# A sign convolution on four 64x64 array tiles, half-image layout and folded norms in a convolution-attention kernel

## The chip, the core and the metric

The kernel runs on one core of one Trainium2 chip. The metric is the time of one execution on the device in microseconds (us), median of several. The engines are TensorE (PE; its weight loads are listed as PEld), VectorE (DVE), ScalarE (ACT), GpSimd (POOL) and SyncE (SP), which issues the DMAs. Each executes its own queue in order and waits for the others by semaphores.

## The reference

Sixteen images of 256 channels and 56x56 positions pass through two layers. `_gn` normalises groups of 8 channels over all positions.

```python
# layer 0: x = x + conv_block(_gn(x))
xq = sign(xn + bias)
out = 0
for i, d in enumerate((1, 3, 5)):                # three dilations
    wq = scale * sign(w[i] - mean(w[i]))         # one scale and mean per output channel
    y = conv3x3(xq, wq, dilation=d, groups=4)    # 64 channels in, 64 out, per group
    y = y + cb[i] - move1[i]
    out += where(y >= 0, y, alpha[i] * y) + move2[i]
out = (out - mean_c(out)) * rsqrt(var_c(out) + 1e-5) * gamma + beta   # over channels
# layer 1: x = x + attention(_gn(x))
q, k, v = 1x1 convolutions of xn, 64 channels each (8 heads of 8)
k, v = unfold3x3(k) + depthwise3x3(k) + biases, same for v            # 9 neighbours
att = softmax over the 9 neighbours of sum_c(q * k)
out = proj(sum over neighbours of att * v), 64 -> 256 channels
```

## The kernel before

An image lies in SBUF as two chunks of 128 channels (`KC`), 3136 positions each, in f32. `front` (L228) takes the group statistics of an image, writes (x - mean) * r on DVE (L238) and its sign on ACT (L246) into two zero-bordered bf16 images `sgn`. `layer0` goes through 7 tiles of 8 rows (448 positions). `conv_tile` (L249) makes, for each chunk and dilation, 9 matmuls (one a tap, L263) of a 128x128 block-diagonal weight matrix (two of the four groups) into one PSUM bank; ACT evacuates it twice with Relu (`up` L272, `dn` L276), DVE combines these into the PReLU (L279), and POOL adds the three dilations (L283, L284). `post` works one tile behind: `centre` (L286) makes the channel mean with a 1/256 matrix (`lmp` L291), subtracts it (L295), squares on ACT (L299) and sums the squares into one row of a PSUM bank for up to four tiles (`lvp` L300). After the fourth and the seventh tile `residual` (L308) takes the root of a 4x448 tile (L199 to L205), spreads each row over 128 partitions by a matmul (`lrp` L315), multiplies (L317), applies gamma and beta on ACT (L318), adds to the image on POOL (L326) and takes the statistics for layer 1 (L328).

`qkv_tile` (L360) normalises the image again on DVE (L365) and makes q, k and v (`qps` L378) with the top half of the image on partitions 0 to 63 and the bottom half on 64 to 127; ACT evacuates (L387, L392). `layer1` has 7 tiles of 4 rows in each half. `attn_weights` multiplies q with 9 shifted k (L412, two on DVE and one on POOL), makes the scores (`lg` L427) and the softmax; `attn_out` transposes (`tp` L454), copies (`at` L460), makes the weights of the shifted v (`ap` L467), multiplies with v (L477), adds on POOL (L491 to L493), projects (`op` L498) and adds to the image (L507).

All PSUM tiles come from one pool of 8 banks (`bank`). Tile pools set how many buffers of a kind there are: 3 images, 6 `ct`, 10 `y` (448 columns, used by nine kinds of tile), 6 `p`. The instructions are put into each engine's queue by a planner, which follows the order of the program by priority and puts an instruction earlier where it expects an engine to wait. An f32 matmul appears in the trace as two passes, each with its weight load.

The images are one layer apart. In step b the program has, in order: load of image b+2, `layer0` of image b+1 (with the q/k/v of image b put in ahead of the last tile's norm), `front` of image b+2, and `layer1` of image b with its store.

Of the kernel before, what the change touches and what calls it, by code (L numbers as in the profile page):

```python
# [7 lines left out]
F32 = mybir.dt.float32  # L8
# [5 lines left out]
P = 128  # L14
C, H, W = 256, 56, 56
HW = H * W
KC = C // P                 # channel chunks of 128
DIL = (1, 3, 5)
PADC = 5                    # zero border of the sign image: the largest dilation
HP = H + 2 * PADC  # L20
TR = 8                      # image rows of a convolution tile
TN = TR * W                 # 448 positions
NT = H // TR                # 7 tiles
LNB = 4                     # tiles whose channel-norm variances are worked on together
NH, CH = 8, 8               # attention heads, channels of a head
D = NH * CH                 # 64
HH = H // 2                 # rows of a half image: partitions 0-63 hold the top half, 64-127 the bottom
AR = 4                      # rows of an attention tile, in each half
AN = AR * W                 # 224 positions
NAT = HH // AR              # 7 tiles  # L30
BN = 2 * W                  # 112 positions: one stationary block of the scores' product
HJ = NH * 9                 # 72 scores of one position
# [4 lines left out]
# columns of the packed per-channel parameters  # L37
# [4 lines left out]
def _view(ap, dims, offset=0):  # L42
    """The partitions of `ap` with other free dimensions (step, count), from its start on."""
    return bass.AP(ap.tensor, ap.offset + offset, [ap.ap[0], *dims])
# [3 lines left out]
def preact_conv_attention(  # L48
# [4 lines left out]
    par: bass.AP,  # L53
    wqkv: bass.AP,
# [8 lines left out]
    bsel: bass.AP,  # L63
# [11 lines left out]
    xpool = ctx.enter_context(tc.tile_pool(name="x", bufs=3))  # L75

    def load(b):
        xt = xpool.tile([P, KC, HW], F32, tag="x", name="xt")
        for k in range(KC):
            nc.sync.dma_start(  # L80
                out=xt[:, k, :], in_=x[b, k * P : (k + 1) * P].rearrange("p h w -> p (h w)")
            )
        return xt

    # ------------------------------------------------------------------ constants and weights
    cst = const.tile([P, 3 * P + LNB * LNB], F32, name="cst")
    nc.sync.dma_start(out=cst, in_=consts)
    ident = cst[:, 0:P]
    gmat = cst[:, P : 2 * P]            # 1/8 within a group of 8 channels
    cmean = cst[:, 2 * P : 3 * P]       # 1/256 everywhere  # L90
    vsel = [cst[:, 3 * P + LNB * t : 3 * P + LNB * (t + 1)] for t in range(LNB)]
    bsl = const.tile([LNB, LNB, P], F32, name="bsl")
    nc.sync.dma_start(out=bsl, in_=bsel)
    pr = const.tile([P, KC, NPAR], F32, name="pr")
    nc.sync.dma_start(out=pr, in_=par)

    images = {0: load(0)}

    wq = const.tile([P, KC, 3, D], F32, name="wq")
# [7 lines left out]
    wp = const.tile([P, C], F32, name="wp")  # L107
    nc.sync.dma_start(out=wp, in_=wproj)

    wconv = const.tile([P, KC, 3, 9, P], BF16, name="wconv")  # L110
    csc = const.tile([P, KC, 3], F32, name="csc")       # weight scale, and its negative
    ncsc = const.tile([P, KC, 3], F32, name="ncsc")
    cbi = const.tile([P, KC, 3], F32, name="cbi")       # cb - move1, and its negative
    ncbi = const.tile([P, KC, 3], F32, name="ncbi")
    nalpha = const.tile([P, KC, 3], F32, name="nalpha")
    mv2 = const.tile([P, KC], F32, name="mv2")          # sum of move2, less its channel mean
    qbs = const.tile([P, 1], F32, name="qbs")
    wmean = const.tile([P, KC, 3], F32, name="wmean")

    nc.vector.tensor_scalar(qbs, qb[:, 0:1], SCALE, None, ALU.mult)  # L120
# [7 lines left out]
    for k in range(KC):  # L128
        nc.tensor.matmul(
            out=m2p[:, 0:1], lhsT=cmean, rhs=mv2[:, k : k + 1], start=k == 0, stop=k == KC - 1  # L130
        )
    nc.vector.tensor_tensor(mv2, mv2, m2p[:, 0:1].broadcast_to([P, KC]), ALU.subtract)

    with tc.tile_pool(name="prep", bufs=2) as prep:
        # taps + identity (unfold and depthwise convolution are one 9x9 map per channel), biases
# [10 lines left out]
        # binary weights: signs (exact in bf16) as block-diagonal [in, out] matrices, and scales  # L146
        for k in range(KC):
            for d in range(3):
                wt = prep.tile([P, D, 9], F32, name="wt")
                nc.sync.dma_start(  # L150
                    out=wt, in_=w[d, k * P : (k + 1) * P].rearrange("o i a b -> o i (a b)")
                )
                wm = wmean[:, k, d : d + 1]
                nc.vector.tensor_reduce(wm, wt, AX.XY, ALU.add, negate=True)
                nc.vector.tensor_scalar(wm, wm, 1.0 / (D * 9), None, ALU.mult)
                ws = csc[:, k, d : d + 1]
                nc.vector.tensor_reduce(ws, wt, AX.XY, ALU.add, apply_absolute_value=True)
                nc.vector.tensor_scalar(ws, ws, 1.0 / (D * 9), None, ALU.mult)
                wz = prep.tile([P, 9, P], F32, name="wz")
                nc.gpsimd.memset(wz, 0.0)  # L160
                for g in range(2):
                    r = slice(g * D, (g + 1) * D)
                    nc.scalar.activation(
                        wz[r, :, r],
                        wt[r].rearrange("o i t -> o t i"),
                        AF.Sign,
                        bias=wmean[r, k, d : d + 1],
                    )
                for t in range(9):
                    tp = bank("wtp")  # L170
                    nc.tensor.transpose(tp[:, 0:P], wz[:, t, :], ident)
                    nc.vector.tensor_copy(wconv[:, k, d, t, :], tp[:, 0:P])
        nc.vector.tensor_scalar(ncsc, csc, -1.0, None, ALU.mult)

    # ------------------------------------------------------------------ working memory
# [10 lines left out]
    cpool = ctx.enter_context(tc.tile_pool(name="c", bufs=6))  # L186
    ypool = ctx.enter_context(tc.tile_pool(name="y", bufs=10))
    ppool = ctx.enter_context(tc.tile_pool(name="p", bufs=6))
    apool = ctx.enter_context(tc.tile_pool(name="a", bufs=2))
    small = ctx.enter_context(tc.tile_pool(name="small", bufs=3))  # L190
    rowp = ctx.enter_context(tc.tile_pool(name="row", bufs=1))

    def ytile(name):
        return ypool.tile([P, TN], F32, tag="y", name=name)

    def rsqrt(pool, v, shape, name):
        """v ** -0.5 for v > 0: square root and reciprocal, then a Newton step to fp32's precision."""
        s = pool.tile(shape, F32, name=f"{name}_s")
        nc.scalar.activation(s, v, AF.Sqrt)  # L199
# [8 lines left out]
    def group_stats(st):  # L208
        """Mean and 1/sqrt(var + eps) of each channel's group, from the channels' bn_stats."""
        mv = small.tile([P, KC, 2], F32, name="mv")  # L210
        for k in range(KC):
            nc.vector.bn_aggr(mv[:, k, :], st[:, k].rearrange("p t s -> p (t s)"))
# [444 lines left out]
```

## Time and profile before

| what | before |
|---|---|
| median of 3 runs | 4715.27 us (4707.69 to 4717.31) |
| span of the profiled execution | 4708.0 us |
| its time outside the span, against the median | about 7 us |
| PE busy | 3666.5 us (78%), 20346 matmul passes |
| DVE / ACT / POOL busy | 2431.7 / 1661.7 / 1552.5 us |
| mean granted TensorE clock | 0.823 |
| convolution matmuls, L263 | 6048, busy 1282.2 us |
| evacuations L272 and L276 | 672 each, busy 485.8 and 480.9 us |
| DMA | 110.36 MB, mean 23 GB/s |

"Busy" is the time in which an engine executes at least one instruction; a wait inside its queue is not busy. A page has six parts: busy shares, the span in 40 slices (digits are tenths), DMA queues, the chain that ended last (followed back from the last instruction), the costliest groups of instructions by line, and DMA issues. The granted clock is the share of full speed that TensorE had; in the trace it is either 1.0 or 0.5 at any time.

### The profile page before, as it was taken

To read this page: it belongs to the slowest core of one execution; us is meant where nothing else is said; L and a number is where in the kernel's file an instruction comes from. 1 tells how busy PE (TensorE), PEld (TensorE's weight loads), DVE (VectorE), ACT (ScalarE), POOL (GpSimd) and SP (SyncE) were. 2 spreads that over 40 slices of the span, in tenths; PEclk is the share of its full clock that TensorE was granted. 3 is DMA by queue.
4 is the path that set the end of the run, shared out by engine and by line. 5 is a ranking of instruction groups with operands and counts; after the bars stand their busy time and mean duration, and the time that the engine had idled before them with its cause. 6 is when DMAs were issued, how large, how long until landed. Compare 5 with 4: busy or idle time off the path is not lost.

```text
span 4708.0 us, 52461 instructions
## 1 busy us (share of the span) xinstructions
PE 3666.5 (78%) x20346; PEld 2262.1 (48%) x20346; DVE 2431.7 (52%) x4472; ACT 1661.7 (35%) x2747; POOL 1552.5 (33%) x1358
## 2 busy tenths in 40 slices
PE   5786877878787787877878778787787877868786
PEld 3345445453553635535354453544545445454565
DVE  6555464554645455464554645546455464553543
ACT  5551441514325153241523505234152441514310
POOL 2333333233333333323333233333333333332333
PEclk8897887978888787887978879788797877978887
DMA  3000101001010010100101001010000101000000
GB/s 118 1 1 1 55 1 55 1 1 55 1 55 1 1 55 1 55 1 1 55 1 55 1 13 43 1 55 1 34 22 1 55 1 55 1 1 28 1 28 28
DMA packets 11657, 110.36 MB, mean 23 GB/s; under 512 B 1532, under 2 KB 2044, under 8 KB 3216
## 3 DMA queue, kind: packets, MB, share of 16 engines
q1 hardware_dynamic: 11408, 107.01, 5.7%
q8 instruction: 160, 2.62, 0.2%
q14 instruction: 89, 0.73, 0.0%
HBM read 55.63 MB, written 51.38 MB: 23 GB/s over the span
## 4 chain that ended last, share of the span: by engine, by line
PE 64%; DVE 16%; POOL 11%; ACT 5%; issue 2%; DMA 0%; POOLq 0%; ACTq 0%; DVEq 0%; SPq 0%
PE cps L263 23%; PE lg L427 14%; PE ap L467 7%; POOL m L491 6%; PE qps L378 5%; PE op L498 4%; PE lvp L300 4%; PE lrp L315 3%; DVE up L279 3%; DVE l_r L201 2%; POOL xt L326 2%; POOL m L492 2%; POOL m L493 2%; DVE m L477 2%; DVE p L412 1%
## 5 line engine op out<-in xcount | busy, mean ns | idle before, releaser
L263 PE MATMUL cps<-sgn,wconv 128*128 128x448 bf16 x6048 | 1282.2, 372 | 8.4 <-ACT sgn L246 8.4
L263 PEld LDWEIGHTS <-wconv 128*128 128x128 bf16 x6048 | 594.1, 100 | 745.1 <-issue 209.0
L279 DVE SCALAR_TENSOR_TENSOR up<-dn,nalpha,up 128x448 f32<-128x448 f32 x672 | 510.7, 766 | 748.2 <-ACT dn L276 745.1
L272 ACT ACTIVATE up<-cps,cbi,csc 128x448 f32<-128x448 f32 x672 | 485.8, 723 | 654.0 <-PE cps L263 653.5
L427 PE MATMUL lg<-wk,p 128*112 128x144 f32 x4032 | 676.3, 334 | 0.9 <-DVE p L412 0.9
L427 PEld LDWEIGHTS lg<-wk,p 128*112 128x112 f32 x4032 | 640.8, 216 | 44.9 <-issue 43.6
L467 PE MATMUL ap<-at,wv 72*64 72x224 f32 x4480 | 558.9, 415 | 73.9 <-ACT at L460 73.9
L460 ACT COPY at<-tp 72x448 f32<-72x448 f32 x112 | 59.1, 527 | 1503.8 <-PE tp L454 1503.8
L283 POOL TENSOR_TENSOR up<-up 128x448 f32<-128x448 f32 x224 | 264.6, 1181 | 902.6 <-DVE up L279 897.6
L498 PE MATMUL op<-m,wp 64*128 64x224 f32 x896 | 209.0, 615 | 372.2 <-POOL m L493 372.2
L276 ACT ACTIVATE dn<-cps,ncbi,ncsc 128x448 f32<-128x448 f32 x672 | 480.9, 716 | 0.0
L467 PEld LDWEIGHTS ap<-at,wv 72*64 72x64 f32 x4480 | 364.2, 160 | 243.0 <-ACT at L460 103.0
L491 POOL TENSOR_TENSOR m<-m 128x448 f32<-128x448 f32 x336 | 379.5, 1129 | 213.3 <-DVE m L477 200.4
L326 POOL TENSOR_TENSOR xt<-xt,ct 128x896 f32<-128x896 f32 x112 | 231.2, 2083 | 650.2 <-ACT ct L318 650.2
L477 DVE TENSOR_TENSOR m<-ap,vt 128x448 f32<-128x448 f32 (+1 forms) x560 | 319.9, 571 | 208.5 <-PE ap L467 171.1
L507 DVE SCALAR_TENSOR_TENSOR xt<-op,pr,xt 128x224 f32<-128x224 f32 x448 | 170.9, 445 | 485.5 <-PE op L498 485.5
L412 POOL TENSOR_TENSOR p<-qt,kt 128x672 f32<-128x672 f32 x112 | 178.8, 1596 | 702.0 <-PE lg L427 643.6
L315 PE MATMUL lrp<-l_r,bsl 4*128 4x448 f32 x224 | 178.4, 970 | 214.0 <-DVE l_r L205 214.0
L498 PEld LDWEIGHTS op<-m,wp 64*128 64x128 f32 x896 | 134.2, 319 | 433.1 <-POOL m L493 427.0
L412 DVE TENSOR_TENSOR p<-qt,kt 128x672 f32<-128x672 f32 x224 | 194.7, 908 | 278.8 <-PE lg L427 159.3
L284 POOL TENSOR_TENSOR ct<-up 128x448 f32<-128x448 f32 x224 | 261.4, 1167 | 141.7 <-DVE up L279 138.6
L378 PE MATMUL qps<-n,wq 128*64 128x224 f32 x2688 | 273.8, 355 | 17.1 <-DVE n L365 17.1
(89 smaller groups left out, 3410.1 us busy)
## 6 DMA issues: line engine op xcount, KB each, us to landing
xt<-in_x SPq DMA_DIRECT2D x32, 1568.0 KB, 9.9
out<-xt SPq DMA_DIRECT2D x32, 1568.0 KB, 5.2
wt<-in_w SPq DMA_DIRECT2D x6, 288.0 KB, 3.3
wk<-in_wk_a SPq DMA_DIRECT2D x1, 720.0 KB, 11.2
kb<-in_wk_b SPq DMA_DIRECT2D x1, 720.0 KB, 12.6
cst<-in_consts SPq DMA_DIRECT2D x1, 200.0 KB
wq<-in_wqkv SPq DMA_DIRECT2D x1, 192.0 KB, 10.1
wv<-in_wv_a SPq DMA_DIRECT2D x1, 180.0 KB
```

Of the source, the lines that this page charges most:

```text
L263: nc.tensor.matmul(out=ps[:, 0:TN], lhsT=wconv[:, k, d, tap, :], rhs=sgn[k][:, r0 : r0 + TR, c0 : c0 + W], start=tap == 0, stop=tap == 8,)
L272: nc.scalar.activation(up, ps[:, 0:TN], AF.Relu, bias=cbi[:, k, d : d + 1], scale=csc[:, k, d : d + 1])
L276: nc.scalar.activation(dn, ps[:, 0:TN], AF.Relu, bias=ncbi[:, k, d : d + 1], scale=ncsc[:, k, d : d + 1])
L279: nc.vector.scalar_tensor_tensor(up, dn, nalpha[:, k, d : d + 1], up, ALU.mult, ALU.add)
L326: nc.gpsimd.tensor_tensor(xv, xv, ct, ALU.add)
L378: nc.tensor.matmul(out=ps[s * D : (s + 1) * D, 0:AN], lhsT=wq[:, k, j, :], rhs=xn[k][:, s * AN : (s + 1) * AN], start=k == 0, stop=k == KC ...
L412: eng.tensor_tensor(p3.rearrange("p d (h w) -> p d h w", w=W), q3.rearrange("p d (h w) -> p d h w", w=W), k3, ALU.mult,)
L427: nc.tensor.matmul(out=lg[0:BN, b * 2 * HJ : (b + 1) * 2 * HJ], lhsT=lhs, rhs=wk[:, j, :], start=j == 0, stop=j == 9,)
L467: nc.tensor.matmul(out=ap[s * D : (s + 1) * D, i * AN : (i + 1) * AN], lhsT=wv[:, j + i, :], rhs=at[:, s * AN : (s + 1) * AN], start=True, ...
L477: nc.vector.tensor_tensor(m[:, 0 : n * AN].rearrange("p (i h w) -> p i h w", h=AR, w=W), ap[:, 0 : n * AN].rearrange("p (i h w) -> p i h w ...
L491: nc.gpsimd.tensor_tensor(ms[0], ms[0], m, ALU.add)
L498: nc.tensor.matmul(out=op[:, k * AN : (k + 1) * AN], lhsT=wp[s * D : (s + 1) * D, k * P : (k + 1) * P], rhs=ms[0][s * D : (s + 1) * D, 0:A ...
```

## The change

*Convolution.* The image is now worked on in strips of 7 rows in both halves (2 x 392 positions), four strips an image. Per chunk, dilation and tap there are four matmuls of 64x64 weights: two groups (rows 0 to 63 or 64 to 127 of the array) times two image halves (columns, so partitions 0 to 63 or 64 to 127 of the output). The result has a group on 128 partitions = 2 halves x 64 channels, so `ct` and the image for the residual are `[128, 4 groups, 1568]`.

*Two copies of the image.* `load_chunks` brings the image by channel chunk for `front`; `load_halves` brings it by half for the residual, after the store of the image whose buffer it takes.

*Norms.* `front` takes the sign of x plus a per-channel shift directly. `layer0` scales the q/k/v weights by the group norm's r and makes a bias from the mean, so `qkv_tile` reads the image itself.

*Channel norm.* Each strip has its own: variances come with positions on the partitions (98 x 8), the root is a power on POOL with a Newton step on DVE, and it is spread by a matmul with the identity.

*Projection.* One 128x128 block-diagonal matmul per group of 64 output channels replaces two 64x128 ones per half.

```diff
-    xpool = ctx.enter_context(tc.tile_pool(name="x", bufs=3))
+    npool = ctx.enter_context(tc.tile_pool(name="xn", bufs=2))
+    xpool = ctx.enter_context(tc.tile_pool(name="x", bufs=2))
...
-    cpool = ctx.enter_context(tc.tile_pool(name="c", bufs=6))
-    ypool = ctx.enter_context(tc.tile_pool(name="y", bufs=10))
-    ppool = ctx.enter_context(tc.tile_pool(name="p", bufs=6))
+    cpool = ctx.enter_context(tc.tile_pool(name="c", bufs=2))
+    upool = ctx.enter_context(tc.tile_pool(name="u", bufs=4))
+    dpool = ctx.enter_context(tc.tile_pool(name="d", bufs=3))
+    qpool = ctx.enter_context(tc.tile_pool(name="q", bufs=1))
+    mpool = ctx.enter_context(tc.tile_pool(name="m", bufs=5))
+    ppool = ctx.enter_context(tc.tile_pool(name="p", bufs=4))
...
     def rsqrt(v, shape, name):
-        s = pool.tile(shape, F32, name=f"{name}_s")
-        nc.scalar.activation(s, v, AF.Sqrt)
-        nc.vector.reciprocal(r, s)
+        nc.gpsimd.tensor_tensor(r, v, h, ALU.pow)        # h: -0.5, broadcast
         nc.vector.tensor_tensor(s, r, r, ALU.mult)
         nc.vector.tensor_tensor(s, s, v, ALU.mult)
         nc.vector.tensor_scalar(s, s, -0.5, 1.5, ALU.mult, ALU.add)
         nc.vector.tensor_tensor(r, r, s, ALU.mult)
...
     def front(xs):
+        # sh = var * r * bias - mean
         for k in range(KC):
-            for t in range(NT):
-                nc.vector.tensor_scalar(n, xt[...], mean, r, ALU.subtract, ALU.mult)
-                nc.scalar.activation(sgn[k][...], n, AF.Sign, bias=pr[:, k, P_BIAS : P_BIAS + 1])
+            for s in range(2):
+                nc.scalar.activation(
+                    sgn[k][:, PADC + s * HH : PADC + (s + 1) * HH, PADC : PADC + W],
+                    xs[k][:, s * HN : (s + 1) * HN].rearrange("p (h w) -> p h w", w=W),
+                    AF.Sign, bias=sh[:, k : k + 1])
...
+    def conv_strip(t):
         for k in range(KC):
             for d, dil in enumerate(DIL):
-                ps = bank("cps")
+                ps = [bank("cps") for _ in range(2)]
                 for tap in range(9):
+                    for j, s in ((0, 0), (1, 1), (0, 1), (1, 0)):
+                        r0 = PADC + s * HH + t * SR + (tap // 3 - 1) * dil
+                        nc.tensor.matmul(
+                            out=ps[j][s * GC : (s + 1) * GC, 0:SN],
+                            lhsT=wconv[j * GC : (j + 1) * GC, k, d, tap, :],
+                            rhs=sgn[k][j * GC : (j + 1) * GC, r0 : r0 + SR, c0 : c0 + W],
+                            start=tap == 0, stop=tap == 8)
+                for j in range(2):
+                    # Relu up, Relu dn on ACT and the PReLU on DVE, per bank of 128x392
             nc.gpsimd.tensor_tensor(es[0], es[0], es[1], ALU.add)               # 128x784
+            nc.gpsimd.tensor_tensor(ct[:, 2 * k : 2 * k + 2, :], es[0], es[2], ALU.add)
...
+    def channel_norm(ct, t, xt, st):
+        # mean: 4 matmuls with 1/256 within a half; 4 subtractions on DVE
+        nc.scalar.activation(sq, ct, AF.Square)                                 # 128x1568
+        for i in range(NVB):                                                    # 4 blocks of 98
+            for g in range(NG):
+                nc.tensor.matmul(out=vp[0:VB, 2 * i : 2 * i + 2],
+                    lhsT=sq[:, g, i * VB : (i + 1) * VB], rhs=hsel, ...)
+        nc.vector.tensor_scalar(v, vp[0:VB, 0 : 2 * NVB], EPS_LN, None, ALU.add)
+        r = rsqrt(v, [VB, 2 * NVB], "l")
+        nc.vector.tensor_copy(rr, r broadcast to [VB, 2 * NVB, GC])
+        for i in range(NVB):
+            nc.tensor.matmul(out=rp[:, i * VB : (i + 1) * VB],
+                lhsT=rr[:, i], rhs=ident[0:VB, 0:VB], start=True, stop=True)
+        nc.vector.tensor_tensor(ct, ct, rp broadcast over 4 groups, ALU.mult)
+        # gamma and beta: 4 on ACT; add to the image on POOL, 128x1568; 4 bn_stats
...
     def layer0(xt, before_tail=None):
+        for t in range(NS):
+            ct = conv_strip(t)
+            if t == NS - 1 and before_tail:
+                before_tail()
+            if last is not None:
+                channel_norm(last, t - 1, xt, st)
+            last = ct
+        channel_norm(last, NS - 1, xt, st)
+        mean, _, r = group_stats(st, NG, gmat1)
+        for g in range(NG):
+            nc.gpsimd.tensor_scalar(wf[:, g], wq[:, g], r[:, g : g + 1], 0.0, ALU.mult, ALU.add)
+        # bp: 24 matmuls of wf (64 columns) with half the mean; bf = qb - bp
...
+    def qkv_tile(xt, wf, bf, t):
+        for g in range(NG):
+            for s, j in ((0, 0), (1, 0), (0, 1), (1, 1)):        # q and k: four 64x64 tiles
+                nc.tensor.matmul(out=pq[s][c * D : (c + 1) * D, 0:AN],
+                    lhsT=wf[s * GC : (s + 1) * GC, g, j, :], rhs=xt[s * GC : (s + 1) * GC, g, pos], ...)
+        for g in range(NG):
+            for s in range(2):                                   # v: two 64x64 tiles
+                nc.tensor.matmul(out=pv[s][s * D : (s + 1) * D, 0:AN], ...)
+        # six evacuations of 64x224 on ACT
...
-        for s in range(2):
+        for g0 in range(0, NG, 2):
             op = bank("op")
-            for k in range(KC):
+            for i in range(2):
                 nc.tensor.matmul(
-                    lhsT=wp[s * D : (s + 1) * D, k * P : (k + 1) * P],
-                    rhs=ms[0][s * D : (s + 1) * D, 0:AN],
+                    lhsT=wp[:, g0 + i, :],
+                    rhs=ms[0][:, 0:AN],
...
         layer1(b, xt)
+        if b + 2 < NB:
+            images[b + 2] = load_halves(b + 2)
```

The preparation also transposes the sign weights four to a bank, copies only their 64x64 blocks, and brings the weight scales into the half layout by eight small DMAs.

## The prediction

> **What bounds the kernel now.** I read the page first: which engine is full, and whether one is full all the time.
>
> ```profile
> PE 3666.5 (78%) x20346; PEld 2262.1 (48%) x20346; DVE 2431.7 (52%) x4472; ACT 1661.7 (35%) x2747; POOL 1552.5 (33%) x1358
> PEclk8897887978888787887978879788797877978887
> PE 64%; DVE 16%; POOL 11%; ACT 5%; issue 2%; DMA 0%; POOLq 0%; ACTq 0%; DVEq 0%; SPq 0%
> PE cps L263 23%; PE lg L427 14%; PE ap L467 7%; POOL m L491 6%; PE qps L378 5%; PE op L498 4%; PE lvp L300 4%; PE lrp L315 3%; DVE up L279 3%; DVE l_r L201 2%; POOL xt L326 2%; POOL m L492 2%; POOL m L493 2%; DVE m L477 2%; DVE p L412 1%
> ```
>
> TensorE carries the chain, but convolution matmuls are only 23% of it, so halving them cannot halve anything. Next I cut one image into stages at the first and last matmul of each kind: convolutions with their norms, q/k/v, the rest of the channel norm, attention.
>
> ```profile
> 1082.00:1197.50 115.50, 102.60 (x428) 44.69 (x426) 59.87 (x91) 67.87 (x103) 38.71 (x30) 0.91 0.14 56
> 1197.50:1215.50 18.00, 17.04 (x169) 12.92 (x169) 10.75 (x16) 10.85 (x25) 5.87 (x4) 1.00 0.01 2
> 1215.50:1245.40 29.90, 13.21 (x31) 5.70 (x31) 20.81 (x43) 8.12 (x15) 6.19 (x3) 0.66 0.00 0
> 1245.40:1369.00 123.60, 92.91 (x646) 74.91 (x647) 58.46 (x125) 16.24 (x30) 46.30 (x47) 0.78 0.00 1
> ```
>
> Columns: length, then busy time of PE, PEld, DVE, ACT, POOL, clock, DMA share, GB/s. Stage 1 is TensorE's, at a good clock; stage 3 is one dependency chain; stage 4 is TensorE with waits, at clock 0.78. Sum 287 us, sixteen times, plus the start. Last, the prices, from the timeline:
>
> ```profile
> 1104.64 1.66 PE L291 MATMUL lmp<-ct,cst 128*128 128x448 f32 x4
> 1110.87 11.43 PE L263 MATMUL cps<-sgn,wconv 128*128 128x448 bf16 x54
> 1113.59 0.72 ACT L272 ACTIVATE up<-cps,cbi,csc 128x448 f32<-128x448 f32 x1 [4.71 <-PE cps L263]
> 1114.21 0.72 ACT L276 ACTIVATE dn<-cps,ncbi,ncsc 128x448 f32<-128x448 f32 x1
> ...
> 1223.69 2.94 DVE L201 RECIPROCAL l_r<-l_s 4x448 f32<-4x448 f32 x1 [0.64 <-ACT l_s L199]
> ...
> 1278.24 4.00 PE L467 MATMUL ap<-at,wv 72*64 72x224 f32 x40 [0.62 <-ACT at L460]
> ...
> 1302.64 1.87 PE L498 MATMUL op<-m,wp 64*128 64x224 f32 x8 [3.83 <-POOL m L493]
> ```
>
> 54 convolution matmuls take 11.43 us, the first few at half clock (44 later ones took 8.79 us: 0.20 each). An f32 pass of 448 columns costs 0.415 us (lmp), so 40 passes of 224 columns one by one would be 8.3 us; ap needs 4.00, so two 64-column tiles already run side by side. op does the same with two 64-row tiles: 8 passes in 1.87 us at clock 0.5, where one by one they would be about 3. Two evacuations start 0.62 us apart.
>
> **Convolution.** Now 7 x 54 = 378 matmuls x 0.20 = 75 us of stage 1. Then 4 strips x 54 taps x 4 tiles = 864 matmuls of 392 columns. Four at a time: 216 groups of at least 0.20 x 392/448 = 0.17 us. No row shows four. Above: two at a time 0.35; or TensorE's instruction rate, where the densest row (40 matmuls and 40 weight loads in 4.00 us, 50 ns each) makes eight instructions 0.40. I take 0.20, near the pure column time, since ap and op show both halves of the packing. A strip is then 10.8 us of TensorE.
>
> ACT takes over: 24 evacuations a strip. 448 columns cost 0.62 and 224 columns 0.45, so 392 cost 0.58, and a strip 14.0 us. TensorE binds only from 14.0/54 = 0.26 us a group. Four strips: 56 us of ACT, plus 3 us for the first group of nine taps at half clock.
>
> **Norm per strip.** The batch of up to four tiles with one root is gone; each strip has its own chain, two of them in stage 1 (the other two follow q/k/v). After ACT has caught up: square 1.4 us (0.58 a 448-column square, plus 1120 columns); variance 32 passes that each load 98 columns for a matmul of two: the nearest row is the group statistics, L214, two passes of 128 loaded columns and two streamed in 0.56 us at half clock, the second starting about 0.21 after the first; 98/128 of it is 0.16: 5.1; add, power on POOL, four small DVE steps, copy of 512: 0.25+1+0.75+0.6 = 2.6; broadcast 8 passes x 0.21 = 1.7; first taps of the next strip at half clock 2.9. Sum 13.7. The waiting TensorE instructions hold the next strip's taps behind them; ACT, DVE and POOL then run dry. The trace shows that the planner sometimes puts ten taps into such a wait, sometimes none; I take none here. The power has no row: 0.16 (a 128x2 DVE step) to 3 us (as long as the reciprocal it replaces); I take 1, nearer a small step. Gone: reciprocal 2.94, square root and its ACT table loads.
>
> Stage 1: 3 + 56 + 2 x 13.7 = 86 us by ACT, less the 7 us that ACT is behind when q/k/v starts (three of the four bank pairs, 2.3 us each): 79, now 115.5. With taps in all waits 68; at 0.35 a group TensorE binds: 76 + 2 x 12 = 100; at 0.40, 110.
>
> **q/k/v.** No normalise (14 x 0.42 us of DVE, hidden under TensorE) and no wait for it, but half the contraction: 16 matmuls for q and k in fours, 8 for v in twos, two passes each: 16 steps of 0.19 (ap: 20 steps and a drain in 4.00) = 3.0 us a tile against 2.3; 42 evacuations of 0.45 instead of 21 keep just under that (19 us). 21 us plus 3 for ACT's backlog = 24, now 18. If f32 passes pair only by twos: 32.
>
> **Tail.** Two norms one behind the other, then statistics and the fold. Two means 5.8, centring 2.2 and square 1.4 partly inside: variance starts at 6.7; two variances to 16.9; second root 19.5; broadcast 21.2; multiply 1.7; scale 4 x 0.66; add on POOL 3.5 (2.08 per 896 columns); statistics 1.9; group statistics 4 (as now); weights on POOL 2; 48 bias passes at 0.1 = 5. Sum 41 against 29.9; 33 if attention's first scores are issued ahead of the fold, 45 with a 3 us power. In the trace they come after the last statistics matmul, so I keep 41.
>
> **Attention.** Scores and values are untouched. The projection becomes block-diagonal 128x128: its 8 passes no longer pair. It sits on the chain behind POOL's adds, at half clock: 8 passes of twice 0.19 = 3.0 us instead of 1.87. The clock comes back at its own time, so work pushed past that costs full-clock time: 0.75 to 1.5 us a tile, 1.0 taken, 7 us an image. Four product buffers instead of six let fewer products run ahead: 0 to 1.5 us a tile, 0.5 taken, 3.5. One ACT table load (1.28) off the chain. 123.6 + 9 = 133 (128 to 140).
>
> **Hidden.** The image is read twice. The second read waits for the store: today the load is issued 9 us after the store and lands 10 us later, and the first add comes some 40 us into stage 1; without that cover POOL's add and the two strip buffers behind it wait a few us. The sign's normalise goes from DVE (14 x 0.42) under the scores. Start: 36 copies for 54, nothing I price.
>
> Sum: 79 + 24 + 41 + 133 = 277 against 287: 10 to 11 us x 16 = 170 us. Span 4708.0 becomes 4538; the median lies 7 above the span: 4545.
>
> **A page against a row.** In the ap stretch the weight loads are busy 2.78 of 4.00 us under matmuls of the same 72 rows, and the pace stays that of the columns. The Trainium skill, "TensorE: Matmul & The Clock Gate", Part 3, says that a weight load overlaps running matmuls only in another row group; with its load time of columns/1.2 ns a group would, by my estimate, be 0.17 + 0.05 = 0.22 us. The row contradicts the rule, and by either ACT still binds.
>
> **Rivals.** *Tiles not four abreast* (slower side): matmuls pair by twos, or instructions bound, at 0.35 to 0.40 us. For: no row shows four, and ap's 50 ns an instruction is the fastest sustained rate. Against: two-fold rows and columns both work. Break-even: the other stages are 198, so stage 1 may take 89, and (89 - 2 x 12)/216 = 0.30 us. At 0.35: 100 + 198 = 298, 11 us worse, 4715 + 176 = 4890; at 0.40 with the bad end of q/k/v, 316: 5180.
> *Waits filled*: the planner fills the norm's waits: 68 + 22 + 34 + 129 = 253: 4715 - 16 x 34 = 4170. For: ten taps in the trace. Against: none ahead of L315 now.
> *The chain costs more than the array saves*: a 3 us power and POOL or DVE queues ahead of each link, 5 us more on four chains: 297, 4870.
>
> **Chances.** Forecast 0.42 (4400 to 4680); filled waits 0.20; tiles not abreast 0.25; chain 0.10; a sum of zero 0.03. Faster 0.62, same 0.03, slower 0.35; 0.2% (9 us) is about what a measurement of this kernel tells from no change. The range 4200 to 4930 leaves out the extremes of the filled and unabreast cases.
>
> **What would show it.** Right: groups of four cps starts within some 20 ns every 0.2 us; ACT up and dn back to back in stage 1; TensorE idle before the variance and broadcast matmuls; op near 3 us; no L201. Wrong: cps groups over 0.30 us; power over 3 us; POOL's add waiting for a load; attention longer than 140.

## The result, and the profile after

The changed kernel takes 5012.57 us (median of its runs, 5011.12 to 5016.22) against 4711.52 us on the same chip: 1.0641 times the time before, 95% interval 1.0625 to 1.0656. The forecast was 4545 us, range 4200 to 4930: wrong in sign, and outside the range.

The page of the changed kernel, its lines of busy time, granted clock and chain:

```profile
PE 3388.8 (68%) x33534; PEld 2671.6 (53%) x33534; DVE 2371.3 (47%) x4280; ACT 1677.4 (33%) x2893; POOL 1677.4 (33%) x1279
PEclk7677778777787777878868788777877778777787
PE 42%; ACT 22%; DVE 14%; POOL 13%; issue 7%; DMA 1%; POOLq 0%; DVEq 0%; ACTq 0%; SPq 0%
PE lg L492 12%; PE ap L532 8%; PE op L563 7%; ACT up L314 6%; ACT dn L318 6%; PE lvp L346 5%; POOL m L556 5%; DVE up L321 3%; PE lrp L363 3%; ACT ct L374 2%; POOL l_r L241 2%; DVE ct L337 2%; DVE st L384 2%; DVE ct L370 2%; ACT kt L456 2%
```

TensorE has 278 us less to do than before, and no other engine has become full: ScalarE has 16 us more and GpSimd 125, but each is busy for a third of the span. The convolution's matmuls, 23% of the chain before, are no longer in the list. In their place stand the evacuations on ScalarE (`up`, `dn`) and the links of the channel norm: centring `ct` (L337), variance `lvp`, root `l_r`, broadcast `lrp`, multiply (L370) and scale (L374). A kernel in which no engine is full and the time grows is waiting. Where it waits shows when one image is cut into the same four stages (length, busy time of PE, PEld, DVE, ACT, POOL, clock, DMA share, GB/s):

```profile
1156.90:1250.00 93.10, 63.88 (x961) 43.85 (x960) 54.07 (x72) 55.17 (x92) 33.83 (x16) 0.77 0.34 70
1250.00:1273.90 23.90, 21.51 (x324) 16.16 (x326) 9.35 (x9) 23.17 (x51) 9.48 (x5) 1.00 0.01 2
1273.90:1334.00 60.10, 29.71 (x169) 24.55 (x164) 20.02 (x54) 12.42 (x21) 12.92 (x9) 0.59 0.00 1
1334.00:1464.10 130.10, 97.17 (x649) 81.98 (x650) 62.95 (x129) 12.93 (x18) 47.53 (x49) 0.81 0.07 25
```

The sum is 307.2 us an image instead of 287. Convolutions with their norms got 22 us shorter (115.5 to 93.1), q/k/v 6 longer, the tail twice as long (29.9 to 60.1), attention 6.5 longer: 20 us more, and 16 x 20 = 320 is about the loss (301 measured; start and end were not cut into stages). So the convolution did get faster. The timeline of the first norm gap in stage 1 shows what ate the gain (start, duration, engine, line; in brackets how long the engine had been idle, and what released it):

```profile
1185.31 1.84 POOL L325 TENSOR_TENSOR up<-up 128x784 f32<-128x784 f32 x1 [1.77 <-DVE up L321]
1185.81 2.30 DVE L321 SCALAR_TENSOR_TENSOR up<-dn,nalpha,up 128x392 f32<-128x392 f32 x2 [0.58 <-ACT dn L318]
1185.87 0.98 ACT L318 ACTIVATE dn<-cps,ncbi,ncsc 128x392 f32<-128x392 f32 x1
1188.03 2.21 DVE L337 SCALAR_TENSOR_TENSOR ct<-ct,mv,lmp 128x392 f32<-128x392 f32 x4
1190.28 1.51 ACT L341 ACTIVATE sq<-ct 128x1568 f32<-128x1568 f32 x1 [3.43 <-DVE ct L337]
1191.84 5.49 PE L346 MATMUL lvp<-cst,sq 128*98 128x2 f32 x32 [7.63 <-ACT sq L341]
1197.61 1.65 POOL L241 TENSOR_TENSOR l_r<-lvar,mhalf 98x8 f32<-98x8 f32 x1 [7.22 <-DVE lvar L354]
1200.11 0.43 DVE L358 COPY lrr<-l_r 98x512 f32<-98x512 f32 x1
1200.68 2.00 PE L363 MATMUL lrp<-cst,lrr 98*128 98x98 f32 x8 [3.35 <-DVE lrr L358]
1202.61 11.18 PE L302 MATMUL cps<-sgn,wconv 64*64 64x392 bf16 x216
1202.79 1.79 DVE L370 TENSOR_TENSOR ct<-ct,lrp 128x1568 f32<-128x1568 f32 x1 [2.25 <-PE lrp L363]
1204.61 2.53 ACT L374 ACTIVATE ct<-ct,pr 128x392 f32<-128x392 f32 x4 [12.82 <-DVE ct L370]
1207.04 0.66 ACT L314 ACTIVATE up<-cps,cbi,csc 128x392 f32<-128x392 f32 x1
```

From the centring to the broadcast the chain has one engine at work at a time. TensorE stands 7.63 us at the variance and 3.35 us at the broadcast, and the whole convolution of the next strip (216 matmuls) is queued behind them. It doesn't need the norm at all. ScalarE's last evacuation began at 1185.87, and when nothing holds them they start 0.563 us apart (median), so the next could have begun at 1186.43. It began at 1207.04: a hole of 20.6 us, with only the norm's own square and scale in it. The trace has 32 such holes, two an image, of 20.6 to 20.8 us. The tail has two more of these chains, and they run one after the other:

```profile
1275.37 2.90 PE L333 MATMUL lmp<-ct,cst 128*128 128x392 f32 x8
1283.39 5.49 PE L346 MATMUL lvp<-cst,sq 128*98 128x2 f32 x32 [5.13 <-ACT sq L341]
1292.22 2.00 PE L363 MATMUL lrp<-cst,lrr 98*128 98x98 f32 x8 [3.34 <-DVE lrr L358]
1294.02 5.02 PE L333 MATMUL lmp<-ct,cst 128*128 128x392 f32 x8
1303.26 5.49 PE L346 MATMUL lvp<-cst,sq 128*98 128x2 f32 x32 [4.23 <-ACT sq L341]
1312.10 2.00 PE L363 MATMUL lrp<-cst,lrr 98*128 98x98 f32 x8 [3.34 <-DVE lrr L358]
```

The second norm's means (`lmp` at 1294.02) begin only when the first norm's broadcast is through, though their input had long been there (GpSimd, which writes it, had been idle for 24.5 us by 1289.17). Over the whole kernel TensorE's waits read (line, released by: us in total, times, longest):

```profile
PE lvp L346 <- ACT sq L341: 454.9, 64, 10.4
PE op L563 <- POOL m L558: 429.0, 112, 5.0
PE lrp L363 <- DVE lrr L358: 213.9, 64, 3.4
```

64 is four norms in each of 16 images. The same two waits in the kernel before:

```profile
PE lrp L315 <- DVE l_r L205: 214.0, 32, 6.7
PE lvp L300 <- ACT sq L299: 111.7, 65, 3.0
```

The first and third row above are 669 us, 42 us an image; before they were 326. TensorE's work on the convolution fell by 598 us (1282.2 to 683.8), and its waits in the norms grew by 343, all of it at the variance. These are TensorE's waits and not yet a loss: where TensorE is ahead of ScalarE, it would have waited in any case. What they cost the experiments have to show.

**Theory T**: each strip's norm is queued whole on an in-order TensorE, four times an image, and its dependency chain holds the convolution (stage 1) or the other norm (tail) behind it. **Rival A**: the evacuations, now in smaller pieces and with VectorE held up under GpSimd's long additions, cost the time. **Rival B**: the block-diagonal projection and the smaller pools in attention cost it.

### The profile page after: what moved, and what is told of

It reads as the page before. It is cut to its first block, busy times and chain, and to the rows that moved or that the text cites. A ratio compares the mean times of both kernels' runs of the same rounds, so it can differ in the third digit from the quotient of the medians.

```text
span 5009.3 us, 78318 instructions
## 1 busy us (share of the span) xinstructions
PE 3388.8 (68%) x33534; PEld 2671.6 (53%) x33534; DVE 2371.3 (47%) x4280; ACT 1677.4 (33%) x2893; POOL 1677.4 (33%) x1279
## 4 chain that ended last, share of the span: by engine, by line
PE 42%; ACT 22%; DVE 14%; POOL 13%; issue 7%; DMA 1%; POOLq 0%; DVEq 0%; ACTq 0%; SPq 0%
PE lg L492 12%; PE ap L532 8%; PE op L563 7%; ACT up L314 6%; ACT dn L318 6%; PE lvp L346 5%; POOL m L556 5%; DVE up L321 3%; PE lrp L363 3%; ACT ct L374 2%; POOL l_r L241 2%; DVE ct L337 2%; DVE st L384 2%; DVE ct L370 2%; ACT kt L456 2%
## 5 line engine op out<-in xcount | busy, mean ns | idle before, releaser
L321 DVE SCALAR_TENSOR_TENSOR up<-dn,nalpha,up 128x392 f32<-128x392 f32 x768 | 776.0, 1052 | 271.3 <-ACT dn L318 266.6
L302 PE MATMUL cps<-sgn,wconv 64*64 64x392 bf16 x13824 | 683.8, 354 | 75.2 <-issue 36.2
L563 PE MATMUL op<-m,wp 128*128 128x224 f32 x896 | 372.2, 597 | 429.0 <-POOL m L558 429.0
L346 PE MATMUL lvp<-cst,sq 128*98 128x2 f32 x2048 | 349.4, 306 | 454.9 <-ACT sq L341 454.9
L314 ACT ACTIVATE up<-cps,cbi,csc 128x392 f32<-128x392 f32 x768 | 576.0, 750 | 189.2 <-PE cps L302 189.2
L346 PEld LDWEIGHTS lvp<-cst,sq 128*98 128x98 f32 x2048 | 343.9, 287 | 496.1 <-ACT sq L341 496.1
L302 PEld LDWEIGHTS <-wconv 64*64 64x64 bf16 x13824 | 426.8, 112 | 326.6 <-issue 109.8
L318 ACT ACTIVATE dn<-cps,ncbi,ncsc 128x392 f32<-128x392 f32 x768 | 580.1, 755 | 45.9 <-DVE up L321 42.7
L563 PEld LDWEIGHTS op<-m,wp 128*128 128x128 f32 x896 | 280.8, 328 | 503.0 <-POOL m L558 478.5
L374 ACT ACTIVATE ct<-ct,pr 128x392 f32<-128x392 f32 x256 | 161.8, 702 | 818.5 <-DVE ct L370 818.5
L325 POOL TENSOR_TENSOR up<-up 128x784 f32<-128x784 f32 x128 | 247.3, 1932 | 453.4 <-DVE up L321 453.4
## 6 DMA issues: line engine op xcount, KB each, us to landing
wq<-in_wqkv SPq DMA_DIRECT2D x1, 384.0 KB, 10.8
```

The costliest lines, as they stand in the source:

```text
L302: nc.tensor.matmul(out=ps[j][s * GC : (s + 1) * GC, 0:SN], lhsT=wconv[j * GC : (j + 1) * GC, k, d, tap, :], rhs=sgn[k][j * GC : (j + 1) * ...
L314: nc.scalar.activation(u, ps[j][:, 0:SN], AF.Relu, bias=cbi[:, g, d : d + 1], scale=csc[:, g, d : d + 1])
L318: nc.scalar.activation(dn, ps[j][:, 0:SN], AF.Relu, bias=ncbi[:, g, d : d + 1], scale=ncsc[:, g, d : d + 1])
L321: nc.vector.scalar_tensor_tensor(u, dn, nalpha[:, g, d : d + 1], u, ALU.mult, ALU.add)
L346: nc.tensor.matmul(out=vp[0:VB, 2 * i : 2 * i + 2], lhsT=sq[:, g, i * VB : (i + 1) * VB], rhs=hsel, start=g == 0, stop=g == NG - 1,)
L374: nc.scalar.activation(ct[:, g, :], ct[:, g, :], AF.Identity, bias=pr[:, g, P_BETA : P_BETA + 1], scale=pr[:, g, P_GAMMA : P_GAMMA + 1],)
```

## The experiments

Medians are compared with the kernel before on the same chip (4711, 4709 and 4713 us in the three batches) and with the changed kernel's 5012.6.

**1. The two norms of the tail side by side.** Their steps are the same, in another order: the means and squares of the two norms alternate with their variances and roots, and both broadcasts come last. `channel_norm` becomes a generator that stops after each of its pieces; `next` runs one piece.

```diff
+            if t == NS - 1:
...
+                a = channel_norm(last, t - 1, xt, st)
+                b = channel_norm(ct, t, xt, st)
+                for n in (a, a, b, a, b, b, a, b):       # means, squares, variances, then the rest
+                    next(n, None)
...
-        channel_norm(last, NS - 1, xt, st)
```

> The changed kernel, but the last two strips' norms go side by side after q/k/v: both means, squares and variances first, then the two broadcasts. Theory (the loss is the per-strip norm chain, queued whole on TensorE, four times an image): the second chain of the tail, now 18 us behind the first, comes 6 to 8 us behind it; stage 3 falls from 60 to about 48 us, the time from 5013 to 4820 (4760 to 4880). Rival A (smaller evacuations and DVE steps held up by POOL cost the time) and rival B (the block-diagonal projection and the small pools cost it): no change beyond 1%.

4807.8 us (4806.5 to 4809.2), ratio 1.0205 (1.0189 to 1.0220). Of the stages only the tail moved by more than 1.2 us:

```profile
1500.60:1524.40 23.80, 21.57 (x325) 16.19 (x327) 9.22 (x9) 23.07 (x50) 9.46 (x5) 1.00 0.01 2
1524.40:1572.10 47.70, 26.08 (x166) 22.26 (x163) 19.76 (x54) 12.35 (x21) 12.90 (x9) 0.61 0.00 1
```

47.7 us instead of 60.1 with the same arithmetic and the same buffers: 205 of the 301 us go with the order of eight steps alone. As T expected.

**2. The chain without its middle.** Square, variance and root are left out, and a constant is spread in place of the root; means, centring, broadcast and scale stay.

```diff
+    rrc = fix.tile([VB, NVB, 2, GC], F32, name="rrc")
+    nc.vector.memset(rrc, 1.0)
...
-        sq = qpool.tile([P, NG, SN], F32, name="sq")
-        nc.scalar.activation(sq, ct, AF.Square)
...
-        r = rsqrt(v, [VB, 2 * NVB], "l")
...
+        rr = rrc
```

> The changed kernel with the square, the variance matmuls and the root left out: a constant is spread by the same broadcast matmuls (the output is not the reference's). Theory: 1.5 + 5.5 + 3.3 us go from each of four chains, 41 us an image, time about 4360 (4250 to 4450). Rival A: stage 1 stays near 90 us since ACT and DVE set it, only the tail gains 20 us: 4690. Rival B: as A.

4171.0 us (4168.1 to 4172.1), ratio 0.8852 (0.8839 to 0.8865), 189 us less time than T expected (4360), and below its range (4250). Stage 1 and tail:

```profile
1201.80:1270.10 68.30, 53.31 (x897) 33.79 (x896) 52.85 (x60) 52.23 (x91) 30.53 (x14) 0.91 0.46 96
1293.80:1325.60 31.80, 14.26 (x104) 11.14 (x101) 17.42 (x42) 9.41 (x19) 9.63 (x7) 0.69 0.00 1
```

25 us of stage 1 and 28 of the tail hang on the middle of the chain, while the evacuations, the additions and the projection that A and B blame are untouched. 22 us of this are the variance's own matmuls (four times 5.49); the other 31 are the square, the root and the waiting for them, which runs 7 to 10 try to cover by a better order. The mean clock of stage 1 rises from 0.77 to 0.91 because long stretches at half clock have gone: in the changed kernel's trace the clock is 0.5 from 1189.21 to 1206.28, over most of the norm's chain and the first taps of the next strip. In the whole kernel the taps gain nothing by it: 1670 of the 13824 take over 0.45 us in the changed kernel, 2206 here (a tap takes 0.33 us at full clock and 0.53 at half).

**3. The projection on four 64x64 tiles** instead of one 128x128 block-diagonal matmul, in the changed kernel.

```diff
-                nc.tensor.matmul(out=op[:, ...], lhsT=wp[:, g0 + i, :], rhs=ms[0][:, 0:AN], ...)
+                for h in range(2):                  # odd groups: the halves change places
+                    c = h if i == 0 else 1 - h
+                    nc.tensor.matmul(out=ops[h][c * GC : (c + 1) * GC, ...],
+                        lhsT=wp[h * GC : (h + 1) * GC, g0 + i, h * GC : (h + 1) * GC],
+                        rhs=ms[0][h * GC : (h + 1) * GC, 0:AN], ...)
```

> The changed kernel with the projection on four 64x64 tiles instead of block-diagonal 128x128 matmuls (the residual adds become eight of 64 partitions instead of four of 128). Theory (the projection costs 0.75 to 1.5 us on the chain of each attention tile, no more): op falls from 3.4 to about 1.9 us, time 4850 to 4930. Rival B (projection is most of the loss): 4700. Rival A: 4850 to 5013.

4919.6 us (4917.0 to 4927.0), ratio 1.0447 (1.0429 to 1.0464). The matmul groups of the changed kernel and of this one (count | busy us, mean ns of one | idle before), and this one's attention:

```profile
L563 PE MATMUL op<-m,wp 128*128 128x224 f32 x896 | 372.2, 597 | 429.0 <-POOL m L558 429.0
```

```profile
L565 PE MATMUL op<-m,wp 64*64 64x224 f32 x1792 | 191.4, 572 | 403.3 <-POOL m L558 403.3
1615.00:1740.10 125.10, 93.73 (x701) 73.44 (x705) 74.83 (x152) 12.93 (x18) 47.52 (x49) 0.77 0.07 27
```

Twice as many matmuls take half the time, 1.6 us less in each of 112 tiles, and 5.0 us an image come off attention (130.1 to 125.1). B is a real cost, 93 us, and not the main one.

**4. Shorter additions on GpSimd**: the 784- and 1568-column ones in pieces of 392.

```diff
-        nc.gpsimd.tensor_tensor(xv, xv, ct, ALU.add)
+        for g in range(NG):
+            nc.gpsimd.tensor_tensor(xv[:, g, :], xv[:, g, :], ct[:, g, :], ALU.add)
```

> The kernel after with its three kinds of long GpSimd additions (784 and 1568 columns) cut into pieces of 392 columns. Theory (the whole chains cost the time, the holding of VectorE under GpSimd's additions a us or two of each gap): 16 x 4 x 0 to 2 us less, 4890 to 5020 us. Rival A (VectorE held under GpSimd's long additions is what costs the time): at most 4750 us.

4925.2 us (4922.6 to 4925.8), ratio 1.0456 (1.0439 to 1.0474): 87 us less, 5.5 an image, most of it from stage 1 (90.7) and the tail (57.9). A too is a real cost of the size that T gave it (it said 0 to 128 us), and far from the 260 us and more that A needed. The gains of runs 1, 3 and 4 add up to 385 us, more than the loss: each is what one part of the changed kernel costs, and they are no shares of the 301.

**5. One array tile at a time**, in the changed kernel: the nine taps of a tile, then the nine of the next.

```diff
-                for tap in range(9):
-                    c0 = PADC + (tap % 3 - 1) * dil
-                    for j, s in ((0, 0), (1, 1), (0, 1), (1, 0)):
+                for j, s in ((0, 0), (1, 1), (0, 1), (1, 0)):
+                    for tap in range(9):
+                        c0 = PADC + (tap % 3 - 1) * dil
```

> The kernel after with its 216 convolution matmuls of a strip in another order: the nine taps of one 64x64 tile, then the nine of the next, so that neighbours in the queue always use the same tile. If the four tiles do run abreast in the kernel after, the convolution now costs TensorE about four times as much: 216 x 0.21 us (the 392-column matmul of the kernel before) = 46 us a strip in place of 11 to 14, 30 us more x 4 x 16 = about 1900 us more, 6900 us (6300 to 7500). If they did not run abreast, the order makes no difference: 4950 to 5100 us.

5487.9 us (two runs, 5486.0 and 5489.8), ratio 1.1653 (1.1630 to 1.1676): between the two expectations. The matmul groups of the changed kernel and of this one:

```profile
L302 PE MATMUL cps<-sgn,wconv 64*64 64x392 bf16 x13824 | 683.8, 354 | 75.2 <-issue 36.2
```

```profile
L302 PE MATMUL cps<-sgn,wconv 64*64 64x392 bf16 x13824 | 1525.4, 349 | 16.0 <-ACT sgn L283 16.0
```

The order is worth a factor of 2.2 of TensorE time, so the tiles do run abreast. It isn't 4, because the queue does not hold a tile's nine taps strictly apart: the starts in the trace show two streams of the same spacing (0.171 us) interleaved for most of a block, the next tile's taps beside the last tile's. My 6900 took them for strictly serial, and at 0.21 us each, which is the pace of a 448-column matmul in the kernel before. In the changed kernel the four starts of a group lie within 10 ns (median), and a group begins every 0.172 us. With TensorE slower, its wait at the variance falls from 454.9 to 250.0 us: 205 us of that wait came with TensorE being faster, and are by themselves no loss.

**6. The kernel before, with a root for every tile** instead of one for four.

```diff
-LNB = 4
+LNB = 1
```

> The kernel before with one edit: its channel norm takes a root for every tile of 448 columns instead of one for four tiles. Theory (each chain of variance, root and broadcast is queued whole on TensorE and stands there, whatever the convolution is like): about five more chains an image at 9 to 13 us each, 16 images, 720 to 1040 us more: about 5570 us (5300 to 5800). Rival (a kernel whose TensorE has other work covers a chain, so that chains are no explanation): within 100 us of the kernel before, about 4750 us.

5531.5 us (5531.0 to 5532.2), ratio 1.1746 (1.1728 to 1.1763), as expected. The two stages that hold norms:

```profile
1628.00:1786.50 158.50, 113.37 (x431) 46.91 (x429) 83.38 (x121) 72.83 (x110) 40.24 (x32) 0.82 0.10 41
1803.80:1843.10 39.30, 14.60 (x30) 5.19 (x29) 24.29 (x45) 7.14 (x14) 4.14 (x2) 0.65 0.00 0
```

Stage 1 grows by 43 us, the tail by 9, and the granted clock of stage 1 falls from 0.91 to 0.82. TensorE's wait at the broadcast rises from 214.0 us (32 times) to 764.6 (112 times). So the price of one more chain, 823/16/5 = 10.3 us, is no matter of the new layout: the old convolution pays it too. Taking fewer, larger norms was the feature of the kernel before that the change gave up.

**7. The norm in four pieces among the next strip's dilations**: means and centring behind its first dilation, square behind the third, variance behind the fourth, broadcast behind the sixth; the last norm's pieces lie between q/k/v tiles. Three `ct` buffers instead of two.

```diff
+            ct = conv_strip(t, lambda u: advance() if u in (0, 2, 3, 5) else None)
+            norms.append(channel_norm(ct, t, xt, st))
...
         for t in range(NAT):
             qkv_tile(xt, wf, bf, t)
+            step()
```

> The changed kernel with the same arithmetic, but each norm in four pieces, put between the dilations of the next strip, and the last strip's between the tiles of q/k/v; a third strip buffer. Theory: stage 1 falls from 93 to 66-70 us (ACT: 96 evacuations at 0.56 us, squares and scales), q/k/v rises from 24 to about 30, the tail falls from 60 to about 25; 4150 (4050 to 4350), below the kernel before. Rival A: the evacuations still take their time and POOL's long adds hold DVE: 4700 to 4800. Rival B: at most the tail gains: 4700.

4431.3 us (4428.7 to 4435.8), ratio 0.9406 (0.9392 to 0.9420): faster than both kernels, and 280 us short of what I expected. The tail has gained more than expected (15.2 us for 25), stage 1 almost nothing (91.6 for 66 to 70). Their rows, and the wait that the timeline shows in stage 1:

```profile
1302.40:1394.00 91.60, 72.09 (x1002) 47.04 (x1001) 55.10 (x87) 62.07 (x103) 38.14 (x19) 0.82 0.34 72
1427.10:1442.30 15.20, 6.85 (x73) 6.02 (x69) 7.37 (x28) 5.35 (x13) 4.47 (x7) 0.72 0.00 1
```

```profile
1322.29 2.98 PE L332 MATMUL lmp<-ct,cst 128*128 128x392 f32 x4 [5.21 <-POOL ct L325]
```

Behind the first dilation of a strip, GpSimd is still adding up the strip before: TensorE stands 5.2 us at the means. The expectation also forgot that a third norm now lies in stage 1. The third strip buffer was not run alone. In the changed kernel the additions that write a strip buffer (L326) wait 109.4 us for VectorE's PReLU and 15.7 for TensorE, about 1 us each, so that two buffers held little up there; and run 1 gained by order alone with two.

**8. The same pieces, each a dilation or more later** (the broadcast behind the second dilation of the strip after next).

```diff
-            ct = conv_strip(t, lambda u: advance() if u in (0, 2, 3, 5) else None)
+            at = {0: (), 1: (2, 3, 5)}.get(t, (1, 2, 3, 5))
+            ct = conv_strip(t, lambda u: advance() if u in at else None)
```

> As the run with the norm in four pieces among the dilations, but each piece a dilation or more later, so that TensorE never comes to a piece before its input is there: strip t has the broadcast of norm t-2 behind its second dilation, then the means, squares and variances of norm t-1 behind the third, fourth and sixth; the last norms lie among the q/k/v tiles. Theory (what is left of the gaps in stage 1 of that run is TensorE waiting at pieces queued too early): stage 1 falls from 92 to 70 to 80 us, the rest stays, 4431 - 16 x 12 to 22 = 4080 to 4240 us. Rival (with the gaps closed stage 1 is bound by the evacuations on ScalarE and VectorE or by the granted clock): 4380 to 4450 us.

4422.7 us (4420.5 to 4431.8), ratio 0.9395 (0.9381 to 0.9409). That is 8.5 us less than run 7 in the median, and the two ranges overlap: no clear change. Stage 1 of one image went from 91.6 to 88.1 us, and the other stages grew by as much (269.7 us an image both times). The total is where the rival put it. But the waits name another reason than the rival's (stage 1 of one image, then TensorE's wait for the square in the whole kernel):

```profile
1290.80:1378.90 88.10, 71.45 (x1001) 48.85 (x1000) 55.26 (x82) 64.99 (x107) 39.42 (x19) 0.81 0.35 75
PE lvp L347 <- ACT sq L341: 10.9, 3, 5.6
PE lvp L347 <- ACT sq L341: 194.6, 47, 7.1
```

The wait for GpSimd is gone from stage 1 (it was 10.8 us there), and TensorE stands at the next link instead: the square is queued on ScalarE behind a dilation's evacuations, and the centring on VectorE behind its own.

**9. The square directly behind the centring, the variance four dilations behind it.**

```diff
-            at = {0: (), 1: (2, 3, 5)}.get(t, (1, 2, 3, 5))
+            at = {2: (t - 1,)} if t else {}        # means, centring, square
+            if t > 1:
+                at |= {0: (t - 2,), 4: (t - 2,)}   # variance; broadcast
```

> The pieces of the norm moved once more: the square is issued directly behind the centring, and the variance's matmuls (which waited 10.9 us of stage 1 for the square in the run before) stand a whole half strip behind it, behind the first dilation of the strip after next; the broadcast three dilations behind that. Theory (what stage 1 has above TensorE's own 71 us is TensorE waiting in its queue for the square): 88 us falls to 75 to 80, 16 x 8 to 13 us less, 4215 to 4295 us. Rival (ScalarE's evacuations, held by VectorE under GpSimd's additions, bind stage 1 by now): 4370 to 4430 us.

4325.3 us (4324.6 to 4327.3), ratio 0.9178 (0.9164 to 0.9192). TensorE's wait for the square falls from 194.6 us in the whole kernel to 5.4. That wait, and stages 1, 2 and 3:

```profile
PE lvp L346 <- ACT sq L340: 5.4, 2, 3.9
1267.30:1341.90 74.60, 64.68 (x970) 40.57 (x970) 49.22 (x73) 55.46 (x92) 34.85 (x17) 0.87 0.42 88
1341.90:1384.10 42.20, 36.37 (x414) 26.73 (x411) 19.55 (x33) 31.35 (x63) 15.61 (x7) 0.92 0.01 1
1384.10:1399.40 15.30, 7.11 (x75) 6.24 (x69) 7.21 (x28) 4.01 (x10) 5.83 (x7) 0.64 0.00 1
```

Stage 1 falls by 13.5 us, just under the low end of what T expected (75); 8 of them come back in q/k/v (33.9 to 42.2), because the 32 variance matmuls of one more norm have been pushed there. The net is 7 us an image, and the total lies between the two expectations (4295 and 4370): the wait was the right one, and moving a piece moves its TensorE time with it.

The order has a second gain, which none of my expectations named. In the changed kernel the variance matmuls come right behind a wait and run at a mean granted clock of 0.51; here they stand between other matmuls, at 0.89, and TensorE needs 222.8 us for them instead of 349.4 (the broadcasts: 0.98 for 0.50, 73.8 us for 127.9).

**10. All three edits together**: the pieces of run 9, the projection of run 3, the additions of run 4.

> The same with two more edits, each run alone before: the output projection on four 64x64 tiles (5 to 6 us an image less in the run that had it alone) and GpSimd's additions in pieces of 392 columns (5 us an image less alone). If they add up: 150 to 190 us below the run with the pieces alone. If the pieces already hide the waits that the short additions took out, 80 to 110 us below it. Before both in either case.

4170.5 us (4168.0 to 4171.5), ratio 0.8847 (0.8833 to 0.8862): the best version, 842 us under the changed kernel. It is 155 us below run 9; the two edits alone gave 93 + 87 = 180, so they nearly add up. One image:

```profile
1223.10:1295.30 72.20, 63.84 (x972) 41.62 (x964) 47.70 (x78) 53.73 (x91) 39.07 (x34) 0.91 0.43 91
1295.30:1335.40 40.10, 36.27 (x410) 26.03 (x412) 18.53 (x35) 31.23 (x59) 18.17 (x17) 0.91 0.01 2
1335.40:1350.90 15.50, 6.90 (x75) 6.04 (x71) 7.08 (x26) 5.63 (x14) 6.11 (x9) 0.72 0.00 0
1350.90:1475.40 124.50, 93.00 (x701) 72.75 (x705) 74.82 (x153) 12.94 (x18) 47.50 (x49) 0.80 0.07 27
```

252 us an image: 55 below the changed kernel, with every norm computed.

## Why the prediction was wrong

**Right.** The four tiles run abreast: a group begins every 0.172 us at full clock where I took 0.20, and a strip's 54 groups take 11.18 us where I had 10.8. The rival that they would not pack, which I gave 0.25, was wrong. ScalarE binds while it has input: evacuations start 0.563 us apart where I had 0.58. q/k/v: 23.9 for 24. The block-diagonal projection: 3.35 us a tile for 3.0. Attention: 130.1 for 133, within the range of 128 to 140; run 3 puts the projection's part at 5 to 6 us an image, where I had 7. No taps filled the waits, as I took it.

**The page against the row.** The Trainium skill, "TensorE: Matmul & The Clock Gate", Part 3, says in its list of what overlaps that a weight load overlaps running matmuls only in another row group (the same Part, on the mechanism, also lets a load for the background weight buffer go ahead). A group of four begins every 0.172 us with four loads of 64 columns, two of them in each row group, where my estimate by the page was 0.22. In run 5 the taps of one and the same tile, each with its load, follow each other at 0.171. The loads are hidden, and the measurement decides against the rule of the list; the sentence on the background buffer agrees with it.

**Wrong, first step: "Norm per strip … Sum 13.7".** The gap is 20.6 us, twice an image: 14 of the 30 us that an image takes over my 277. Left out: the last evacuation's VectorE step, held under a GpSimd addition, and the centring behind it (3.9 us, from 1186.43 to 1190.28; I let the chain begin at the square). The addition of 1185.31 runs to 1187.15, the two PReLU steps beside it to 1188.11. Too small: the end, where multiply and scale stand in front of the next evacuation and not the first taps (4.4 us from 1202.61 to 1207.04, for 2.9), the power (1.65 for 1.0), the variance (5.49 for 5.1) and the broadcast (2.00 for 1.7). 3.9 + 1.5 + 0.65 + 0.4 + 0.3 = 6.8 of the 6.9.

**Wrong, second step: the tail.** I wrote "two means 5.8 … variance starts at 6.7; two variances to 16.9", which is the two norms side by side. The code calls `channel_norm` twice, and TensorE takes its queue in order, so the second norm's means stand behind the first's broadcast. 60.1 us for 41: 19 us an image. (The terms that I listed add up to 41.9, not 41.) Run 1 has the order that I had priced: its tail is 47.7, so 12 of the 19 are the order. The other 7 are links that I sized too small or left out, all of them ahead of the second broadcast: in run 1's trace the first variance starts 9.4 us into the tail and not 6.7; the second square waits for the first variance, because there is one `sq` buffer, and TensorE stands 1.7 us for it; and the second root's last step stands on VectorE behind the first norm's multiply. I read the order of the queue in stage 1, and assumed another in the tail.

14 + 19 - 3 (attention) = 30 us an image, 16 x 30 = 480 us, and 4545 + 480 = 5025 against 5013: the two steps hold the whole miss, within 12 us.

**The rival that came.** "The chain costs more than the array saves", at 0.10 and 4870 us, had the right place and the wrong reasons. Its power of 3 us took 1.65. Its queues on VectorE and GpSimd are there (3.9 us ahead of the square in stage 1), but it left out the largest single term, the order of TensorE's queue in the tail. It put 5 us more on each of four chains, where 7 on two and 19 on the pair in the tail came.

## What to carry to other kernels

When a change makes one resource faster, write down for each in-order engine what is queued behind each wait, before and after; a dependent chain queued whole costs its latency every time it is issued, so count chains and not their arithmetic. Split such a chain into pieces and queue each piece one more unit of independent work later than its input; when a wait moves to the next link, move that link too. When two chains follow each other in the program, price them one after the other unless the code interleaves them.

## What the runs showed of the hardware

**VectorE is held under GpSimd's additions.** In the changed kernel one evacuation's VectorE step, with two inputs in SBUF, beside an addition of 1568 columns:

```profile
1207.21 3.53 POOL L382 TENSOR_TENSOR xt<-xt,ct 128x1568 f32<-128x1568 f32 x1 [7.95 <-ACT ct L374]
1208.30 2.86 DVE L321 SCALAR_TENSOR_TENSOR up<-dn,nalpha,up 128x392 f32<-128x392 f32 x1 [3.73 <-ACT dn L318]
```

The step takes 0.615 us when no GpSimd instruction runs at its start (median of 530); it starts at 1208.30 and ends at 1211.16, 0.42 us behind the end of the addition at 1210.74. 238 of the 768 steps begin under an addition: they take 1.86 us in the median, and end 0.42 us (median) behind it. In all that is 335 us of VectorE more than at 0.615 us a step. The profile shows this as a long busy time of VectorE, not as a wait. Pieces of 392 columns (run 4) bring it to 229 us, and with the pieces of run 10 it is 117. The Trainium skill, "SBUF — State Buffer", section "Who interferes with whom", has the rule: a VectorE instruction with two SBUF inputs and a GpSimd instruction that reads SBUF shut each other out for the whole of an instruction. These rows agree, in the direction where GpSimd came first.

**A power on GpSimd** costs 1.65 us for 98x8, 1.02 for 128x4 and 0.70 for 128x2: about 0.16 us a column on top of 0.4, so the root of a strip (8 columns) costs more than that of the group statistics (4).
